# A two-layer relational graph convolution on one core: layer 1's projections issued in pieces between edge products, and transpositions issued one bunch after the copies they read

## The chip, the cores and the metric

The kernel runs on one core of one Trainium2 chip. The metric is the device time of one execution in microseconds (us). A few terms are used throughout. TensorE is PE in the profile, and PEld is its weight load; VectorE is DVE, ScalarE is ACT, GpSimd is POOL, and SyncE is SP. Each of these engines runs its own instructions strictly in the order in which the program issues them, so an instruction that waits holds back everything behind it on its engine.

## What is computed

There are 12,500 nodes with 128 features each and 200,000 edges sorted by destination. An edge has one of ten relations, the argmax of ten of its attributes. A layer averages the features of the sources over the edges of each (destination, relation) pair, multiplies the average by the relation's 128x128 matrix, sums over relations, and adds a root term and a bias:

```python
seg = dst * NUM_REL + edge_type
sums = segment_sum(x[src], seg); cnt = segment_sum(ones, seg)
mean = (sums / maximum(cnt, 1)).reshape(N, NUM_REL, -1)
return einsum('nrd,rdo->no', mean, w_rel) + x @ root + bias
```

The second layer takes the relu of the first one's result. The output is layernorm(x + layer 2). Everything is in float32.

## The kernel before, in words

**Tiles and bunches.** A tile is 128 edges; there are 1,563 of them (NT). Four tiles (QB) are a bunch, and layer 1's loop at L951 goes over bunches p. For each tile POOL gathers 128 source rows into a buffer `g` (L751); DVE compares keys with a table and writes a one-hot matrix `oh` (L765); ACT scales it by the edge weights (L757); PE multiplies `g` by `oh` into a PSUM tile `zp` (L986); DVE adds `zp` into the accumulator `cc` (L797), which is a ring of 1,024 node columns for each relation and each of two layers. In float32 one product is two PE passes, so the profile counts each twice.

**Both layers at once.** From tile T0 = 177 on, a gathered row holds the node's input features and, where it is already known, its layer-1 result: POOL gathers from one of two tables XH, and each tile is multiplied for both layers (16 passes a bunch). A block of nodes enters a table at an epoch. Epochs are whole multiples of RT = 11 tiles, and the first that lies at least READY = 8 bunches behind the block's finish is taken (L121), so it lies 8.0 to 10.5 bunches behind. The edges whose source is not known in time are done in layer 2 (L1290), which gathers from the finished table `hD`.

**Buffers.** There are 7 buffers `g`, so POOL may stand up to seven bunches ahead of PE. There are five `zp` tiles, two to a bunch. Everything else in PSUM shares two banks (`pf`).

**The order is written by hand.** `todo.at(t, f)` (L804) puts off a step to a later bunch; `todo.run(t)` at the end of a bunch (L1016) issues what is due. Within bunch p the program issues: `ones` of p+2 (DVE), the weights of p+1 (ACT), the gathers of p (POOL), the products of p (PE), pending preparation jobs, the sums of p-2 (DVE), then `finish(k)` for a block of 256 nodes that is now complete, then the steps that are due.

**Finishing a block in layer 1 (L844), about every eight bunches.** With p the bunch of finish, the steps are: in p, `projected` (L732), 11 matmuls of 256 columns, 22 PE passes in a row: ten relations (L739) and the root term (L742). In p+1, ACT copies the result with relu into `a` (L672, issued by L860), PE transposes `a` (L864), ACT copies the transposed rows to `hb` (L871), and SP stores them to `hD` and XH (L634); SP also fetches the next block's features. In p+2 and p+3 ACT clears the block's part of the ring (L722). At the end of p+3 PE runs the second layer's 22 passes; in p+4 ACT copies them to `v` (L891) and PE transposes the next block's features (L919); in p+5 ACT copies those (L926) and clears, and in p+6 it clears again.

**Finishing a block in layer 2 (L1394).** Time is counted in tiles i and a step unit u, which is 0.7 tile for the usual block of 256 nodes: the projection at i; at i+6u ACT's copy `a` (L1416) and, straight after it, PE's transposition (L1423); at i+10u the layernorm (L1427, first instruction L700) and the fetch for the next block.

Of the kernel before, what the change touches and what calls it, by code (L numbers as in the profile page):

```python
# [1 line left out]

# [62 lines left out]
def rgcn_resnorm_kernel(ctx: ExitStack, tc: tile.TileContext, x, src, dst, attr, w_rel1, root1, b1,  # L65
# [122 lines left out]
    def bounds(t):  # L188

        return max(0, t * STEP - OFF, floor_of(t)), min(N - 1, t * STEP + OFF)  # L190
# [541 lines left out]
    def projected(k, l, last, po=None, more=True, ring=None):  # L732
# [9 lines left out]
        nc.tensor.matmul(po[:, :n], w, f[:, :n], start=not more, stop=True)  # L742
        return po

    def stored(hb, b, k):

        rows_dma(hb, XH[b][:, C:], k, True)
# [89 lines left out]
    def layer_1():  # L837

        todo = Later()
        done = 0  # L840
        zps, ohs, xbs, fTs = {}, {}, {}, {}
        offs, row = None, None

        def finish(k, t):  # L844
# [9 lines left out]
            both = starts[k + 1] > bounds(T0)[0] if k + 1 < NBLK else True  # L854
            reused = starts[k] + RN < N
            assert not reused or t + 7 * u <= (starts[k] + RN - OFF - WN) // STEP

            def rows_out(_):
                a = po.pop()
                a = fin_a.setdefault(k, shifted(a, k, 0))  # L860
                pr = ps_f.tile([P, 4, C], F32, name="pf")
                n0, n, subs = block(k)
                for i, h in subs:
                    nc.tensor.transpose(pr[:h, i, :], a[:, i * P:i * P + h], ident)  # L864
                po.append(pr)

            def rows_kept(now):
                pr = po.pop()
                hb = fin.tile([P, 2, C], F32, name=f"hb{k % 2}")
                for p, s in spans(k):  # L870
                    nc.scalar.activation(hb[:p, s], pr[:p, s], AF.Copy)  # L871
                rows_dma(hb, hD, k, True)
                if k <= K1:
                    first = 0 if k <= K0 else (k - K0) % 2
                    free = first_seen[k - 1] - QB if k > K0 else 0
                    if now >= free:
                        stored(hb, first, k)
                    else:
                        todo_late.append((free, lambda t: stored(hb, first, k)))
                    if k < K1:  # L880
                        when = t + 8 * QB if k < K0 else first_seen[k] - QB
                        todo_late.append((when, lambda t: stored(hb, 1 - first, k)))

            def second(_):
                po.append(projected(k, 1, (rsb[1], fin_a.pop(k)), more=both))

            def second_kept(_):
                n0, n, _ = block(k)
                p2 = po.pop()
                t2 = fin.tile([P, 3 * P], F32, name="v")  # L890
                nc.scalar.activation(t2[:, :n], p2[:, :n], AF.Identity, bias=bsb[1])  # L891
                nc.sync.dma_start(T2[:, n0:n0 + n], t2[:, :n])

            todo.at(t + u, rows_out)
            todo.at(t + u, rows_kept)
            if reused:
                todo.at(t + 2 * u, lambda t: cleared(0, k, 0))
                todo.at(t + 3 * u, lambda t: cleared(0, k, 1))
            if k < NBLK - 1:
                todo.at(t + (9 if k >= NBLK - 3 else 3) * u, second)  # L900
                todo.at(t + (9 if k >= NBLK - 3 else 4) * u, second_kept)
            else:
                todo.run(t)
                todo.run(END)
                todo.at(t, second)
                todo.at(t, second_kept)
            if both:
                w = 10 if k >= NBLK - 3 else 5
                todo.at(t + w * u, lambda t: cleared(1, k, 0))
                todo.at(t + (w + 1) * u, lambda t: cleared(1, k, 1))  # L910
            if k + 1 < NBLK - 1:
                def fetch(t):
                    xbs[k + 1] = rows_in(k + 1)

                def turn(t):
                    n0, n, subs = block(k + 1)
                    pt = ps_f.tile([P, YB], F32, name="pf")
                    for i, h in subs:
                        nc.tensor.transpose(pt[:, i * P:i * P + h], xbs[k + 1][:h, i, :], ident[:h, :h])  # L919
# [31 lines left out]
        for p in range(-AHEAD, NPT + BEHIND):  # L951
# [27 lines left out]
            def products(g, oh, slot):  # L979
                t0, n = parts[p]  # L980
                zps[p] = [ps_z.tile([P, YB], F32, name="zp") for _ in range(0, n, 2)]
                for j in range(n):
                    i = t0 + j
                    zp, a = zps[p][j // 2], j % 2 * 2 * KW
                    for l in (0, 1) if i >= T0 else (0,):
                        nc.tensor.matmul(zp[:, a + l * KW:a + (l + 1) * KW], g[:, (slot[j] + l) * C:(slot[j] + l + 1) * C],  # L986
                                         oh[:, j * KW:(j + 1) * KW], start=True, stop=True)

            def sums():
                nonlocal done, offs, row  # L990
# [22 lines left out]
            if p == NPT - 1:  # L1013
                products(*made)
            made = None
            todo.run(t)  # L1016
# [4 lines left out]
        assert not todo_late and not jobs.due  # L1021

    if NCH > 1:
        sources(1)
# [265 lines left out]
    def layer_2():  # L1290
# [103 lines left out]
        def finish(k, i):  # L1394

            todo.run(END)
            fetched(k)
            ring = 1 - walk_of[k]
            n0, n, subs = block(k)
            u = (1 if n > YB * 5 // 8 else 0.7) if i < NG else 0  # L1400
            folded(slice(ring, ring + 1), k, max([b[6] for b, (lo, hi) in zip(bunches, reaches)
                                                  if b[0] == walk_of[k] and lo < n0 < hi] + [WN]))
            po = [projected(k, 1, (ident, fTs[k]), ring=ring)]
            following = turn_of[walk_of[k]]
            if k == partial:
                following = turn_of[1][1:2]
            else:
                following = following[following.index(k) + 1:][:1]
            if k == NB2 - 1:
                following = finals  # L1410
            elif following and following[0] in finals:
                following = []

            def turn(_):
                a = fin.tile([P, 3 * P], F32, name="a")
                nc.scalar.activation(a[:, :n], po.pop()[:, :n], AF.Copy)  # L1416
                if k == partial:
                    nc.sync.dma_start(T2[:, n0:n0 + n], a[:, :n])
                    fetched(following[0])
                    return  # L1420
                pr = ps_f.tile([P, 4, C], F32, name="pf")
                for b, h in subs:
                    nc.tensor.transpose(pr[:h, b, :], a[:, b * P:b * P + h], ident)  # L1423
                po.append(pr)

            def norm(_):
                normed(k, xbs[k], po.pop())  # L1427
                for f in following:
                    fetched(f)

            if k in finals:
                last_steps.extend((turn, norm))
# [12 lines left out]

        fetched(0)
        fetched(partial)
# [264 lines left out]
```

## Time and profile before

| what | value |
|---|---|
| median of 3 runs | 3830.8 us (3828.63 to 3833.66) |
| the profiled execution | 3870.04 us, its span 3868.2 us |
| granted TensorE clock, mean | 0.782 of full speed |
| busy share of the span | PE 63%, POOL 60%, DVE 53%, ACT 34% |
| layer 1 with both tables, 311 to 2406 us | 2095 us, 1,386 gathers |
| layer 2 with its own lists, 2697 to 3784 us | 1087 us, 691 gathers |

The profiled execution is 39 us longer than the median. A group's row gives busy time, mean duration of one in ns, and then the engine's idle time just before these instructions with what ended it. "remote" there, and "another core or an unknown queue" in the chain, stand for a wait whose end the profile cannot attribute.

### The profile page before, as it was taken

To read this page: it belongs to the slowest core of one execution; us is meant where nothing else is said; L and a number is where in the kernel's file an instruction comes from. 1 tells how busy PE (TensorE), PEld (TensorE's weight loads), DVE (VectorE), ACT (ScalarE), POOL (GpSimd) and SP (SyncE) were. 2 spreads that over 40 slices of the span, in tenths; PEclk is the share of its full clock that TensorE was granted. 3 is DMA by queue.
4 is the path that set the end of the run, shared out by engine and by line. 5 is a ranking of instruction groups with operands and counts; after the bars stand their busy time and mean duration, and the time that the engine had idled before them with its cause. 6 is when DMAs were issued, how large, how long until landed. Compare 5 with 4: busy or idle time off the path is not lost.

```text
span 3868.2 us, 42422 instructions
## 1 busy us (share of the span) xinstructions
PE 2449.6 (63%) x11862; PEld 2035.8 (53%) x11862; DVE 2030.8 (53%) x5475; ACT 1306.5 (34%) x3189; POOL 2301.8 (60%) x2443
## 2 busy tenths in 40 slices
PE   1535676767676767676667776245457676665667
PEld 0435665656565656566566666234434444454555
DVE  4435455655455656554444443187556555555565
ACT  1322333333333333333333333122324344444443
POOL 6645666666666666666566665655566666565650
PEclk7657787888888878788788788656678888888778
DMA  4663434343434343434343333211112222221221
GB/s 138 179 183 104 133 107 130 105 129 102 130 107 135 102 130 104 130 106 134 97 131 107 105 97 86 72 45 49 43 49 64 60 60 59 58 60 54 60 61 28
DMA packets 265342, 370.70 MB, mean 96 GB/s; under 512 B 51441, under 2 KB 197398, under 8 KB 265100
## 3 DMA queue, kind: packets, MB, share of 16 engines
q0 software_dynamic: 99968, 250.31, 23.4%
q1 hardware_dynamic: 111517, 91.95, 7.6%
q10 hardware_dynamic: 53615, 25.62, 2.3%
q8 instruction: 102, 1.67, 0.2%
q14 instruction: 140, 1.15, 0.1%
HBM read 322.58 MB, written 57.89 MB: 98 GB/s over the span
## 4 chain that ended last, share of the span: by engine, by line
PE 32%; another core or an unknown queue 22%; DVE 21%; issue 17%; ACT 4%; DVEq 2%; DMA 1%; POOL 1%; ACTq 0%; SPq 0%; POOLq 0%
PE zp L986 13%; PE pf L739 11%; DVE cc L797 8%; PE zp L1505 2%; ACT oh L757 2%; DVE oh L775 2%; DVE oh L765 2%; PE zq L1505 1%; DVEq L782 1%; PE pf L742 1%; PE pf L1197 1%; POOL g L751 1%; ACT cc L722 1%; DVE eqb L548 1%
## 5 line engine op out<-in xcount | busy, mean ns | idle before, releaser
L751 POOL DMA_INDIRECT g<-XH,idxE x1386 | 1311.3, 946 | 815.7 <-issue 387.6
L797 DVE TENSOR_TENSOR cc<-cc,zp 128x240 f32 (+12 forms) x2190 | 836.3, 382 | 1023.7 <-remote 604.5
L986 PE MATMUL zp<-oh,g 128*128 128x120 f32 x5898 | 983.6, 325 | 552.6 <-issue 382.7
L986 PEld LDWEIGHTS zp<-oh,g 128*128 128x128 f32 x5898 | 913.7, 236 | 621.5 <-issue 441.2
L751 POOL DMA_INDIRECT g<-hD,idxB x691 | 653.0, 945 | 433.1 <-issue 194.1
L739 PE MATMUL pf<-cc,w 128*128 128x256 f32 (+5 forms) x3000 | 762.8, 412 | 138.3 <-issue 61.4
L739 PEld LDWEIGHTS pf<-cc,w 128*128 128x128 f32 x3000 | 612.6, 217 | 269.7 <-issue 94.8
L757 ACT ACTIVATE oh<-oh,wE 128x120 f32<-128x120 f32 x1740 | 533.2, 382 | 225.2 <-DVE oh L765 124.0
L757 ACT ACTIVATE oh<-oh,wB 128x150 f32<-128x150 f32 (+23 forms) x771 | 337.9, 481 | 410.4 <-DVE oh L775 198.3
L1505 PE MATMUL zp<-oh,g 128*128 128x120 f32 (+22 forms) x1254 | 341.7, 417 | 211.1 <-DVE cc L797 89.1
L1505 PEld LDWEIGHTS zp<-oh,g 128*128 128x128 f32 x1254 | 239.9, 240 | 289.5 <-issue 239.6
L722 ACT ACTIVATE cc<-zero 128x1280 f32<-128x1280 f32 (+1 forms) x274 | 336.2, 1229 | 74.8 <-DVE cc L797 57.6
L775 DVE TENSOR_TENSOR oh<-wide,keyB 128x480 f32<-128x480 f32 (+19 forms) x402 | 228.8, 569 | 228.8 <-remote 156.0
L672 ACT ACTIVATE a<-pf,b 128x256 f32<-128x256 f32 (+1 forms) x50 | 23.3, 466 | 812.6 <-remote 570.8
L765 DVE TENSOR_TENSOR oh<-bank,keyE 128x480 f32<-128x480 f32 x391 | 253.1, 647 | 0.0
L1505 PE MATMUL zq<-oh,g 128*128 128x140 f32 (+20 forms) x642 | 193.2, 435 | 87.3 <-DVE cc L797 32.7
L751 POOL DMA_INDIRECT g<-hD,idxE x177 | 168.6, 953 | 121.9 <-issue 49.7
L751 POOL DMA_INDIRECT g<-in_x_dram,idxE x177 | 167.3, 945 | 110.0 <-issue 50.8
L1505 PEld LDWEIGHTS zq<-oh,g 128*128 128x128 f32 x642 | 127.2, 234 | 134.5 <-issue 88.2
L797 DVE TENSOR_TENSOR cc<-cc,zq 128x150 f32 (+20 forms) x321 | 124.0, 386 | 55.1 <-PE pf L739 21.3
L891 ACT ACTIVATE v<-pf,b 128x256 f32<-128x256 f32 (+2 forms) x52 | 24.0, 461 | 320.0 <-remote 100.7
L548 DVE TENSOR_TENSOR eqb<-bank,kh 128x1344 bf16<-128x1344 f32 (+2 forms) x65 | 100.5, 1549 | 28.1 <-remote 22.3
(241 smaller groups left out, 1296.2 us busy)
## 6 DMA issues: line engine op xcount, KB each, us to landing
m<-in_edge_attr_dram SPq DMA_DIRECT2D x48, 672.0 KB
g<-XH,idxE POOLq DMA_INDIRECT x1386
XH<-in_x_dram ACTq DMA_DIRECT2D x24, 512.0 KB
XH<-zero ACTq DMA_DIRECT2D x24, 512.0 KB
XH<-hb SPq DMA_DIRECT2D x87, 128.0 KB
g<-hD,idxB POOLq DMA_INDIRECT x691
xb<-in_x_dram SPq DMA_DIRECT2D x72, 128.0 KB
hD<-hb SPq DMA_DIRECT2D x46, 128.0 KB
```

Source lines behind the costliest of these rows:

```text
L548: nc.vector.tensor_tensor(eq[:p], kpP[:p, None, :R].to_broadcast([p, DB, R]), fore, op=ALU.is_equal)
L722: nc.scalar.activation(cc[:, l, h * H:(h + 1) * H, o:o + n], zero[:, None, :n].to_broadcast([P, H, n]), AF.Copy)
L739: nc.tensor.matmul(po[:, :n], wsb[l][:, r, :], cc[:, l if ring is None else ring, r, o:o + n], start=(r == 0), stop=False)
L742: nc.tensor.matmul(po[:, :n], w, f[:, :n], start=not more, stop=True)
L751: nc.gpsimd.indirect_dma_start(out=g[:, j * C:(j + n) * C], out_offset=None, in_=table, in_offset=bass.IndirectOffsetOnAxis(ap=idx, axis=0))
L757: nc.scalar.activation(s, s, AF.Copy, scale=w)
L765: nc.vector.tensor_tensor(o.rearrange("p (t m) -> p t m", m=m), cols[:, None, :m].to_broadcast([P, n, m]), keys[:, :, None].to_broadcast([ ...
L775: nc.vector.tensor_tensor(to, a, b, op=ALU.is_equal)
L782: vals = nc.values_load_multi_w_load_instructions(row, engines=[DVE], min_val=min(a for a, _ in lims), max_val=max(b for _, b in lims), sk ...
L797: nc.vector.tensor_tensor(s, s, z, op=ALU.add)
L986: nc.tensor.matmul(zp[:, a + l * KW:a + (l + 1) * KW], g[:, (slot[j] + l) * C:(slot[j] + l + 1) * C], oh[:, j * KW:(j + 1) * KW], start=Tr ...
L1505: nc.tensor.matmul(zp[:, j * m:(j + 1) * m], gt[:, b * C:(b + 1) * C], oh[:, j * m:(j + 1) * m], start=True, stop=True)
```

## The change

No instruction is added or taken away; instructions change places on PE, ACT, SP and DVE.

- Layer 1's projections (both layers' parts, for every block that is kept for two layers except the last three) are cut into 11 pieces of two passes. Three are issued where all 11 stood. Of the rest, two each go behind the first and the second tile's products of the next bunch, and the last four at that bunch's end, ahead of its due steps.
- In layer 1 the copy `a` stays in p+1, but the transposition, the copy to `hb` and the stores move from p+1 to p+2 (not for the last block but one). The transposition of the next block's features moves from p+4 to p+5, and its copy from p+5 to p+6.
- In layer 2 the copy stays at i+6u, the transposition moves to i+8u, and the layernorm from i+10u to i+11u.

```diff
+    def projection(k, l, last, po, more=True):
+        n0, n, _ = block(k)
+        o = n0 % RN
+        def piece(r):
+            if r is None:
+                w, f = last()
+                nc.tensor.matmul(po[-1][:, :n], w, f[:, :n], start=not more, stop=True)
+            else:
+                if not r:
+                    po.append(ps_f.tile([P, YB], F32, name="pf"))
+                nc.tensor.matmul(po[-1][:, :n], wsb[l][:, r, :], cc[:, l, r, o:o + n], start=(r == 0), stop=False)
+        return [piece_of(piece, r) for r in [*range(NREL), None]]
...
+        def beside(pieces, t):
+            now = 3 if t + 2 * QB < NT else len(pieces)
+            for f in pieces[:now]:
+                f()
+            if pieces[now:]:
+                side[t // QB + 1] = pieces[now:]
...
-            po = [projected(k, 0, (rsb[0], fTs[k]))]
+            apart = both and k < NBLK - 3
+            if apart:
+                po = []
+                beside(projection(k, 0, lambda: (rsb[0], fTs[k]), po), t)
+            else:
+                po = [projected(k, 0, (rsb[0], fTs[k]))]
...
+            def rows_copied(_):
+                a = po.pop()
+                fin_a[k] = shifted(a, k, 0)
+
             def rows_out(_):
-                a = po.pop()
-                a = fin_a.setdefault(k, shifted(a, k, 0))
+                a = fin_a[k]
...
-            def second(_):
+            def second(t):
+                if apart:
+                    beside(projection(k, 1, lambda: (rsb[1], fin_a.pop(k)), po), t)
+                    return
...
-            todo.at(t + u, rows_out)
-            todo.at(t + u, rows_kept)
+            todo.at(t + u, rows_copied)
+            todo.at(t + (1 if k == NBLK - 2 else 2) * u, rows_out)
+            todo.at(t + (1 if k == NBLK - 2 else 2) * u, rows_kept)
...
-                w = 2 if k == NBLK - 3 else 4
+                w = 2 if k == NBLK - 3 else 5
                 todo.at(t + w * u, turn)
                 todo.at(t + (w + 1) * u, turned_kept)
...
+                pieces = side.pop(p, [])
                 for j in range(n):
...
+                    if j < 2:
+                        for f in [pieces.pop(0) for _ in range(min(2, len(pieces)))]:
+                            f()
+                left.extend(pieces)
...
             made = None
+            while left:
+                left.pop(0)()
             todo.run(t)
...
-            def turn(_):
+            def copied(_):
                 a = fin.tile([P, 3 * P], F32, name="a")
                 nc.scalar.activation(a[:, :n], po.pop()[:, :n], AF.Copy)
...
+                po.append(a)
+
+            def turn(_):
+                a = po.pop()
                 pr = ps_f.tile([P, 4, C], F32, name="pf")
...
-            todo.at(min(i + 6 * u, by), turn)
+            todo.at(min(i + 6 * u, by), copied)
...
-                todo.at(i + 10 * u, norm)
+                todo.at(i + 8 * u, turn)
+                todo.at(i + 11 * u, norm)
```

More of the change, by code (lines that the diff above doesn't have):

```diff
@@ L1 @@
 from contextlib import ExitStack
+from functools import partial as piece_of
 import concourse.bass as bass
@@ L840, in layer_1 @@
         done = 0
-        zps, ohs, xbs, fTs = {}, {}, {}, {}
+        zps, ohs, xbs, fTs, side = {}, {}, {}, {}, {}
         offs, row = None, None
+        left = []
+        def beside(pieces, t):
[3 more added lines that the diff above has]
+            if pieces[now:]:
+                assert t // QB + 1 not in side
+                side[t // QB + 1] = pieces[now:]
         def finish(k, t):
             if k < NBLK - 2:
+                while left:
+                    left.pop(0)()
                 todo.run(END)
@@ L852, in finish @@
             folded(ALL, k, WN)
-            po = [projected(k, 0, (rsb[0], fTs[k]))]
             both = starts[k + 1] > bounds(T0)[0] if k + 1 < NBLK else True
+            apart = both and k < NBLK - 3
+            assert not apart or t + 4 * QB < NT
+            if apart:
[3 more added lines that the diff above has]
+                po = [projected(k, 0, (rsb[0], fTs[k]))]
             reused = starts[k] + RN < N
             assert not reused or t + 7 * u <= (starts[k] + RN - OFF - WN) // STEP
+            def rows_copied(_):
+                a = po.pop()
+                fin_a[k] = shifted(a, k, 0)
             def rows_out(_):
-                a = po.pop()
-                a = fin_a.setdefault(k, shifted(a, k, 0))
+                a = fin_a[k]
                 pr = ps_f.tile([P, 4, C], F32, name="pf")
@@ L1015, in layer_1 @@
             made = None
+            while left:
+                left.pop(0)()
             todo.run(t)
@@ L1020, in layer_1 @@
         todo.run(END)
-        assert not todo_late and not jobs.due
+        assert not todo_late and not jobs.due and not side
     if NCH > 1:
@@ L1431, in finish @@
             if k in finals:
-                last_steps.extend((turn, norm))
+                last_steps.extend((copied, turn, norm))
                 if k == finals[1]:
```

## The prediction

> **What bounds the kernel now.** I read the page's busy times first, then the chain that ended last.
>
> ```profile
> span 3868.2 us, 42422 instructions
> PE 2449.6 (63%) x11862; PEld 2035.8 (53%) x11862; DVE 2030.8 (53%) x5475; ACT 1306.5 (34%) x3189; POOL 2301.8 (60%) x2443
> PE 32%; another core or an unknown queue 22%; DVE 21%; issue 17%; ACT 4%; DVEq 2%; DMA 1%; POOL 1%; ACTq 0%; SPq 0%; POOLq 0%
> PE zp L986 13%; PE pf L739 11%; DVE cc L797 8%; PE zp L1505 2%; ACT oh L757 2%; DVE oh L775 2%; DVE oh L765 2%; PE zq L1505 1%; DVEq L782 1%; PE pf L742 1%; PE pf L1197 1%; POOL g L751 1%; ACT cc L722 1%; DVE eqb L548 1%
> ```
>
> No engine is full, and the chain wanders between PE, DVE and releasers that the trace cannot name. The change touches two stages, so I cut them out by windows (window and length, then busy time with instructions of PE, PEld, DVE, ACT and POOL, granted clock, DMA share, GB/s).
>
> ```profile
> 311.00:2406.00 2095.00, 1455.42 (x7866) 1271.02 (x7867) 1060.96 (x2814) 670.56 (x1740) 1310.76 (x1386) 0.82 0.39 115
> 2697.00:3784.00 1087.00, 694.76 (x2631) 514.85 (x2629) 614.97 (x1788) 450.43 (x956) 653.02 (x692) 0.79 0.21 57
> ```
>
> In the first, which is layer 1 for both tables, PE is busy for 1455 of 2095 us (69%). POOL shows 1311 us, but its sequencer needs time between two gathers. What POOL waited for in this window (total us, times, longest):
>
> ```profile
> POOL g L751 <- issue: 387.6, 1205, 3.5
> POOL g L751 <- remote: 215.9, 100, 3.9
> POOL g L751 <- PE zp L986: 87.1, 37, 6.7
> POOL g L751 <- DMA XH<-hb: 35.6, 8, 9.0
> POOL g L751 <- DMA XH<-zero: 31.9, 1, 31.9
> POOL g L751 <- PE pf L742: 21.2, 11, 2.6
> POOL g L751 <- PE pf L864: 16.0, 4, 9.6
> POOL g L751 <- PE pf L559: 7.2, 5, 1.9
> POOL g L751 <- PE pf L269: 7.1, 3, 3.0
> POOL g L751 <- PE pf L919: 2.6, 1, 2.6
> ```
>
> The issue row is 1,205 gaps of 0.32 us. Busy time and issue together are 1698 us, 81% of the stage: POOL is the nearest thing to a bound, and the other 397 us are its pauses. 141.2 us of them (the five rows that name PE) wait for PE to release a `g`; 215.9 us end at something unnamed; 35.6 us wait for a block's rows to reach the table XH. In layer 1, therefore, a change of PE's order is worth only what it takes from, or adds to, these pauses. PE's own idle time costs nothing as long as POOL does not pause for it.
>
> **A, the projections in pieces.** One block in the timeline (start, length, engine, line, idle time before and its releaser):
>
> ```profile
> 1204.36 6.77 PE L739 MATMUL pf<-cc,w 128*128 128x256 f32 x20
> 1211.40 1.94 PE L986 MATMUL zp<-oh,g 128*128 128x120 f32 x16
> 1221.91 0.94 POOL L751 DMA_INDIRECT g<-XH,idxE  x1 [2.95 <-remote]
> 1222.01 0.69 PE L864 MATMUL pf<-ident,a 128*128 128x128 f32 x2 [8.68 <-DVE cc L797]
> 1227.86 4.48 PE L739 MATMUL pf<-cc,w 128*128 128x256 f32 x20
> 1249.47 3.74 PE L986 MATMUL zp<-oh,g 128*128 128x120 f32 x16 [0.95 <-issue]
> ```
>
> The 20 relation passes take 4.48 to 6.77 us in a row, where a bunch's 16 products take 1.94 to 3.74 us; POOL behind the burst paused for 2.95 us. The change spreads 88 such projections (two of each of 44 blocks). No pass is saved. Of 22 passes 14 now stand ahead of or between the next bunch's products and 8 behind them, so that these products end 8/22 = 36% of a burst earlier. What pauses do the bursts cause? The rows that name a projection or the transposition behind it are 21.2 + 16.0 = 37.2 us, 26% of the 141.2 us. If the unnamed pauses have the same share, 0.26 x 215.9 = 57 us, all bursts together cost 94 us. I take 36% of that: **-34 us**, with the bounds 0 and -94. Seven buffers `g` speak for the low end, since 5.0 us of gathers a bunch can run ahead of a burst; they are full wherever POOL waits for PE.
>
> **B, ACT's order.** These rows price what moves.
>
> ```profile
> L739 PE MATMUL pf<-cc,w 128*128 128x256 f32 (+1 forms) x1760 | 453.3, 412 | 47.0 <-issue 32.5 <-ACT v L891 9.1 <-DVE oh L765 1.2
> L722 ACT ACTIVATE cc<-zero 128x1280 f32<-128x1280 f32 (+1 forms) x169 | 210.3, 1246 | 55.3 <-DVE cc L797 49.3 <-issue 6.0
> L864 PE MATMUL pf<-ident,a 128*128 128x128 f32 x87 | 24.6, 373 | 107.0 <-DVE cc L797 73.3 <-ACT a L672 13.5 <-issue 11.7
> L919 PE MATMUL pf<-ident,xb 128*128 128x128 f32 x87 | 19.6, 309 | 14.3 <-ACT v L891 10.6 <-DVE cc L797 3.6
> PE zp L986 <- ACT oh L757: 66.1, 29, 5.5
> ```
>
> With the copy `hb` moved to p+2, it and the clear (1.25 us) stand together ahead of the weights of a bunch that PE will multiply next. PE waited for such weights 29 times in some 346 bunches, 8%. 44 blocks x 8% x 1.25 us is **+5 us**; the bounds are 0 (ACT is busy for 32% of the stage and catches up) and 44 x 1.25 = +55.
>
> PE's 107.0 us ahead of the transposition (L864) look like the prize, but I price them at nothing. Before, the burst ends bunch p, the products of p+1 follow, and then the transposition waits for the copy `a`. After, the last four pieces end bunch p+1, the products of p+2 follow, and then comes the transposition. One bunch of products stands between, now as then. What these waits cost POOL is the row of 16.0 us, which is in A's bound. The copy's own order does not change: `a` stays behind the same products.
>
> **C, the table XH.** `hb` and its stores come a bunch of products later: 1.94 us at full clock to 3.74 us, in the mean 2.9 us. Does a gather stand behind that? Blocks of rows enter the table 8.0 to 10.5 bunches behind their finish. By the kernel's own lists 14 of the 41 epochs lie under 9 bunches behind, and the pauses are found with these. Three of them, with the windows of 32 gathers around them and three windows of 32 without one:
>
> ```profile
> 1321.02 0.95 POOL L751 DMA_INDIRECT g<-XH,idxE  x1 [6.74 <-PE zp L986]
> 1853.30 0.95 POOL L751 DMA_INDIRECT g<-XH,idxE  x1 [8.73 <-DMA XH<-hb]
> 2188.46 0.95 POOL L751 DMA_INDIRECT g<-XH,idxE  x1 [9.01 <-DMA XH<-hb]
> ```
>
> ```profile
> 1793.50:1839.80 46.30, 32.94 (x192) 30.05 (x190) 30.51 (x80) 15.80 (x40) 30.36 (x32) 0.82 0.46 136
> 1827.30:1881.50 54.20, 37.02 (x196) 32.12 (x195) 27.56 (x66) 16.83 (x44) 30.55 (x32) 0.78 0.34 96
> 1262.30:1309.50 47.20, 36.54 (x208) 30.73 (x207) 31.33 (x92) 15.58 (x40) 30.27 (x32) 0.89 0.37 104
> 1298.00:1349.10 51.10, 35.45 (x187) 30.42 (x188) 27.71 (x81) 15.57 (x40) 30.27 (x32) 0.77 0.35 97
> 2128.60:2174.70 46.10, 35.67 (x188) 30.79 (x188) 19.16 (x46) 15.95 (x41) 30.25 (x32) 0.79 0.36 103
> 2162.30:2216.60 54.30, 36.19 (x168) 29.84 (x167) 24.23 (x59) 15.69 (x40) 30.25 (x32) 0.73 0.37 104
> ```
>
> The three waits, less the usual 0.30, are 23.6 us; their windows are 7.9 + 3.9 + 8.2 = 20.0 us longer than those without. So 85% of such a wait becomes time. 14 blocks x 2.9 us x 0.85 is **+35 us**. The bounds are 0 (the stores land in time) and a whole bunch of the stage, 2095 us / 346.5 = 6.05 us, for the 16 epochs that lie up to 9 bunches behind: 97 us.
>
> **D, the next block's features.** PE's 14.3 us ahead of L919 are mostly a wait for the copy `v` (10.6), which a bunch of distance covers. PE is not the bound, so I take a third: **-5 us**, bounds 0 and -14. The copy `fT` is needed only at the next finish, two bunches later.
>
> **E, layer 2.** Here copy and transposition stood back to back, and PE waited.
>
> ```profile
> PE pf L1423 <- ACT a L1416: 82.1, 15, 12.9
> L700 DVE TENSOR_TENSOR v<-pf,xb 128x256 f32<-128x256 f32 x20 | 8.4, 420 | 35.7 <-PE pf L1423 13.3 <-PE zp L1505 9.7 <-remote 7.6
> ```
>
> Two steps u are 1.4 tiles, at 1087 us / 691 gathers = 1.57 us a tile 2.2 us. 15 waits x 2.2 us = 33 us go from PE's path. Some of these waits are 12.9 us long and only shrink, and what is late next is PE's wait for DVE's sums, so I take half: **-16 us**, bounds 0 and -82. The layernorm keeps 3 steps u instead of 4 behind the transposition; DVE already idles 35.7 us there, which bounds the loss at +36.
>
> **The sum** is -34 + 5 + 35 - 5 - 16 = -15 us: layer 1 stays as it is (+1), layer 2 gains 16. The profiled execution is 3870.0 us, 39.2 us above the median of the runs shown; I carry the difference over: 3830.8 - 15 = **3816 us**.
>
> **The rivals.**
>
> R1, slower: the stores decide. If the stores slip a whole bunch of the loop, with PE's transposition held behind products that themselves wait and ACT's `hb` behind them, all 16 epochs pay 6.05 us x 0.85 = +82; the bursts are worth half of my figure (-17). With B, D and E as above: 82 - 17 + 5 - 5 - 16 = +49, **3880 us**. It turns to a loss from a delay of 50 / (14 x 0.85) = 4.2 us, as all other terms sum to -50. For it speaks that XH waits up to 9.0 us already exist; against it, that most epochs lie over 9 bunches behind.
>
> R2, no change: only the pauses that name a burst are its doing. A is 36% of 37.2, -13: the sum is +6, **3837 us**. The many unnamed releasers speak for this: a pause that begins after PE is done is not cured by a smoother PE.
>
> R3, much faster: the bursts start all their pauses and a step of distance cures layer 2's waits (A -94, E -33): -94 + 5 + 35 - 5 - 33 = -92, **3739 us**. Against it: the seven buffers.
>
> R4, slower by the clock. The same 20 passes took 6.77 us in one place and 4.48 us in another, with a granted clock of 0.82 for the stage: the pace of PE varies. If cutting the bursts puts all 88 projections at the slower pace, that is 2.29 x 88 = 201 us of PE; at PE's 32% of the chain, +64 us, and the sum is +49: **3880 us**. Against it: PE's busy share does not change, and single passes between products leave no new gap. The Trainium skill, "TensorE: Matmul & The Clock Gate", section "HAM oscillation — how this bites in real kernels", holds that idle gaps of more than about 3.4 us halve PE's rate again and advises to keep its work together, which would favour the burst. The trace leaves that open: the slow products of 3.74 us show only 0.95 us of idle time ahead of them.
>
> That the change does not do what it says is no rival: in the instruction order of the changed program the pieces, transpositions and copies stand where the diff puts them.
>
> **How the numbers follow.** The forecast has 0.36, with 3786 to 3823 as its own range (A from -27 to -64 with the rest as taken), R1 0.30, R2 0.14, R3 0.12, R4 0.08. About 0.2%, 7.7 us, is what a measurement can tell from no change. Faster is forecast and R3, 0.48; within it R2, 0.14; slower R1 and R4, 0.38. The range, 3755 to 3895, takes in the forecast, R2 and most of R1 and R4 (each some 15 us to either side), and leaves out R3 and their tails.
>
> **What would show it.** In layer 1's POOL waits, A: the rows naming L742 and L864 fall from 37 us by about a third, and the unnamed one with them. C: the row of XH<-hb rises from 35.6 us (8 waits) to some 70. B: PE's wait for ACT's weights stays near 66. D: PE's wait for `v` ahead of L919 goes. PE's idle time ahead of L864 stays near 107. E: the wait for L1416 falls from 82 to about 49, and layer 2 is some 16 us shorter. I am wrong if layer 1's length moves by more than 50 us, or if PE's passes change their mean of 412 ns.

## The result

| | median us | lowest to highest | runs |
|---|---|---|---|
| before | 3831.43 | 3828.63 to 3833.66 | 7 |
| after | 3844.97 | 3840.07 to 3849.43 | 7 |

The change costs 13.5 us: the ratio is 1.0034, with a 95% interval of 1.0024 to 1.0044. The forecast was 3816 us, 15 us faster: 3845 us lies inside its range of 3755 to 3895 us, but the sign is wrong. In a second comparison (run after_again below) the same two kernels took 3865.84 and 3893.89 us: ratio 1.0074 (1.0059 to 1.0088), 28 us slower.

Two things have to be known before the profiles are compared. The levels of separate comparisons differ, here by 34 us for the kernel before, so a kernel is judged only against the runs of the kernel before in its own comparison. And the profile of before shown above took 3870.0 us, 39 us over the median that goes with it, but only 4 us over the 3865.84 of the second comparison. I therefore set it beside the profile of after_again (3886.76 us, where the runs' median is 3893.89) and not beside the first profile of after (3840.07 us).

The windows of the same two stages in after_again, from the first to the last gather out of XH and from layer 2's first to its last gather (columns as before):

```profile
303.00:2430.80 2127.80, 1491.38 (x7854) 1279.83 (x7854) 1056.53 (x2803) 659.98 (x1724) 1310.85 (x1386) 0.81 0.39 113
2725.00:3801.30 1076.30, 697.14 (x2628) 514.78 (x2626) 614.07 (x1781) 449.58 (x955) 652.53 (x691) 0.79 0.22 57
```

POOL's 1,386 gathers take the same 1311 us, but the stage is 2127.8 us long and was 2095. Layer 2's gathers take 1076.3 us and took 1085.7 (2697.35 to 3783.08). So the loss is in layer 1, in what POOL waits for (from 311 us on, so that the wait for the first table, 32.5 us until 303 us, is not among the rows):

```profile
POOL g L768 <- issue: 398.5, 1213, 6.6
POOL g L768 <- remote: 227.0, 96, 4.5
POOL g L768 <- PE zp L1028: 113.3, 46, 11.3
POOL g L768 <- DMA XH<-hb: 64.0, 13, 10.6
POOL g L768 <- PE pf L754: 4.8, 3, 2.4
POOL g L768 <- PE pf L901: 2.2, 2, 1.9
...
POOL g L768 <- PE pf L758: 1.4, 1, 1.4
```

The rows that name the projection (L754 and L758 now) and its transposition (L901) have shrunk from 37.2 us to 8.4 us, as the change would have it, while the products' own row has grown from 87.1 to 113.3 us and the unnamed one from 215.9 to 227.0. The row of the tables has grown from 35.6 us in 8 waits to 64.0 us in 13. The names are only the last releasers, so I also took the pauses by place: for every gather of this stage the idle time ahead of it less 0.31 us, from the trace's list of gathers. At the first gathers of the 41 epochs they sum to 90 us before and 140 us in after_again (49 more); everywhere else to 302 and 287 (15 less). Of the 49 us, 28 lie at the 14 epochs that are under 9 bunches behind (83 us for 55), 21 at the 26 others (24 for 3) and 1 at the first one, where POOL waits for the new table (32 in both). The longest pause behind the first table's belonged to the epoch of the prediction's row at 1853.30 us, where it was 8.73 us:

```profile
1870.44 0.95 POOL L768 DMA_INDIRECT g<-XH,idxE  x1 [10.63 <-DMA XH<-hb]
```

Why the rows come later can be seen in one block of after_again, at the place where the prediction showed the burst of before. Some rows of PE, the copies and the store are shown; `...` stands for rows left out.

```profile
1205.32 1.47 PE L758 MATMUL pf<-cc,w 128*128 128x256 f32 x6
...
1210.73 0.70 PE L758 MATMUL pf<-cc,w 128*128 128x256 f32 x2 [0.33 <-issue]
...
1211.45 0.60 PE L1028 MATMUL zp<-oh,g 128*128 128x120 f32 x4
...
1211.89 1.04 PE L758 MATMUL pf<-cc,w 128*128 128x256 f32 x4
...
1212.76 1.05 PE L1028 MATMUL zp<-oh,g 128*128 128x120 f32 x8
...
1213.65 1.47 PE L758 MATMUL pf<-cc,w 128*128 128x256 f32 x6
...
1214.95 0.59 PE L754 MATMUL pf<-fT,root 128*128 128x256 f32 x2
...
1223.35 0.47 ACT L673 ACTIVATE a<-pf,b 128x256 f32<-128x256 f32 x1 [19.76 <-remote]
...
1223.88 0.69 PE L901 MATMUL pf<-ident,a 128*128 128x128 f32 x2 [2.98 <-ACT a L673]
...
1224.91 0.38 ACT L908 ACTIVATE hb<-pf 128x256 f32<-128x256 f32 x1
...
1225.74 0.46 SPq L635 DMA_DIRECT2D XH<-hb  x1
```

In before, the root term that ends the burst of the prediction's row at 1204.36 us, and the copy behind it:

```profile
1210.96 0.59 PE L742 MATMUL pf<-fT,root 128*128 128x256 f32 x2
...
1221.49 0.47 ACT L672 ACTIVATE a<-pf,b 128x256 f32<-128x256 f32 x1 [23.05 <-remote]
```

In after_again the projection's first pass starts at 1205.3 and its last one (the root term) ends at 1215.5: the whole next bunch lies inside it. In before the burst began at 1204.4 and ended at 1211.5. The copy `a` reads the last pass, so it now follows the end of bunch p+1. Over the 41 blocks that have an epoch, from the trace's lists of these instructions: the mean time from the last product of bunch p to the copy `a` is 12.4 us before and 16.0 us in after_again (1.3 and 6.3 us behind the last product of p+1); the mean time from the last gather of bunch p to the first store into XH is 46.0 and 49.1 us.

### The profile page after: what moved, and what is told of

It reads as the page before. It is cut to its first block, busy times and chain, and to the rows that moved or that the text cites. A ratio compares the mean times of both kernels' runs of the same rounds, so it can differ in the third digit from the quotient of the medians.

```text
span 3838.2 us, 42453 instructions
## 1 busy us (share of the span) xinstructions
PE 2485.1 (65%) x11862; PEld 2036.8 (53%) x11862; DVE 2031.1 (53%) x5475; ACT 1299.9 (34%) x3189; POOL 2300.0 (60%) x2443
## 4 chain that ended last, share of the span: by engine, by line
PE 35%; DVE 19%; issue 18%; another core or an unknown queue 18%; ACT 6%; DVEq 2%; POOL 1%; DMA 1%; ACTq 0%; SPq 0%; POOLq 0%
PE zp L1028 15%; PE pf L758 8%; DVE cc L814 7%; PE pf L740 5%; ACT oh L774 3%; PE zp L1558 2%; DVE oh L792 2%; ACT cc L723 2%; POOL g L768 1%; DVE oh L782 1%; PE zq L1558 1%; DVEq L799 1%; PE pf L754 1%; DVE cc L1213 1%
## 5 line engine op out<-in xcount | busy, mean ns | idle before, releaser
L1028 PE MATMUL zp<-oh,g 128*128 128x120 f32 x5898 | 1016.6, 322 | 555.6 <-issue 416.8
L1028 PEld LDWEIGHTS zp<-oh,g 128*128 128x128 f32 x5898 | 938.5, 233 | 674.6 <-issue 497.1
L758 PE MATMUL pf<-cc,w 128*128 128x256 f32 (+1 forms) x1760 | 526.1, 430 | 107.8 <-issue 59.0
L758 PEld LDWEIGHTS pf<-cc,w 128*128 128x128 f32 x1760 | 358.6, 224 | 171.6 <-issue 81.2
L1558 PEld LDWEIGHTS zp<-oh,g 128*128 128x128 f32 x1254 | 240.9, 241 | 311.7 <-issue 220.5
L740 PE MATMUL pf<-cc,w 128*128 128x256 f32 (+7 forms) x1240 | 316.5, 419 | 86.8 <-DVE cc L814 36.7
```

What stands on the lines that cost most here:

```text
L740: nc.tensor.matmul(po[:, :n], wsb[l][:, r, :], cc[:, l if ring is None else ring, r, o:o + n], start=(r == 0), stop=False)
L758: nc.tensor.matmul(po[-1][:, :n], wsb[l][:, r, :], cc[:, l, r, o:o + n], start=(r == 0), stop=False)
L1558: nc.tensor.matmul(zp[:, j * m:(j + 1) * m], gt[:, b * C:(b + 1) * C], oh[:, j * m:(j + 1) * m], start=True, stop=True)
```

## The experiments

Two theories were set against each other. **S**: what costs is that a block's rows reach XH later, so that the first gather of an epoch waits. **P**: cutting the projections costs by itself, in the order of PE or ACT. A third, **L**, looked for the loss in layer 2. Each kernel was timed in five rounds beside the kernel before; its ratio is to the runs of before in the same comparison.

### The parts, first time

Layer 2's part alone was the changed kernel with

```diff
-            apart = both and k < NBLK - 3
+            apart = False
-            todo.at(t + (1 if k == NBLK - 2 else 2) * u, rows_out)
-            todo.at(t + (1 if k == NBLK - 2 else 2) * u, rows_kept)
+            todo.at(t + u, rows_out)
+            todo.at(t + u, rows_kept)
-                w = 2 if k == NBLK - 3 else 5
+                w = 2 if k == NBLK - 3 else 4
```

> Layer 2's part of the change alone (copy at i+6u, transposition at i+8u, layernorm at i+11u); layer 1 as before. Theory S (the stores to XH that come a bunch later cost what the other parts gain, and more): layer 2 gains its estimated 16 us, 3815. Theory P (cutting the projections is what costs): 3815 too. Theory L (the later layernorm and the lost distance to the next block are what costs): 3840 or more.

Layer 1's part alone took back layer 2's timing:

```diff
-                todo.at(i + 8 * u, turn)
-                todo.at(i + 11 * u, norm)
+                todo.at(min(i + 6 * u, by), turn)
+                todo.at(i + 10 * u, norm)
```

> Layer 1's part of the change alone (pieces, later transpositions and stores); layer 2 as before. Theory S and theory P: the whole loss and layer 2's gain on top, 3831 + 13 + 16 = 3860. Theory L: 3831 or less.

The pieces alone kept `apart` and took back all the rest, which is the last two changes of the first diff and the whole second one:

> Only the projections in pieces: copy, transposition, copy to hb and stores all in p+1 behind the last piece, so that the transposition again waits for its copy. Theory S: no later stores than before by more than the last eight passes, 3820 to 3835. Theory P: 3850 to 3860.

And the later transpositions alone set `apart = False` and took back layer 2's timing:

> Only layer 1's transpositions a bunch later (block's rows, with copy hb and stores, and the next block's features); projections in one burst, layer 2 as before. Theory S: +35 to +45, about 3870. Theory P: 3825 to 3835, since the transposition no longer waits for its copy.

All four missed, in the same way. They took 3087.93, 3089.84, 3090.07 and 3088.79 us, and the kernel before took 3089.07 us beside them (ratios 0.9996, 1.0005, 1.0007 and 0.9999, and each interval takes in 1). Everything, the kernel before included, was 742 us faster here than in the first runs. The waits of POOL in l2_only, in the stage with the tables, show why:

```profile
POOL g L768 <- issue: 381.7, 1253, 0.3
POOL g L768 <- PE zp L1028: 24.4, 80, 0.3
POOL g L768 <- DMA g<-XH,idxE: 9.4, 31, 0.3
```

No wait is longer than 0.3 us: POOL never pauses, and the stage's window is its gathers, 1,386 at 1.25 us:

```profile
225.30:1958.60 1733.30, 1432.66 (x7943) 1241.34 (x7944) 1058.77 (x2820) 667.61 (x1733) 1311.37 (x1386) 0.85 0.47 138
```

With POOL as a bound that never waits, no order on the other engines can show. To see whether the chip or the kernels had done it, the changed kernel itself was run again.

> The changed kernel itself again. In the four runs before, POOL issued a gather every 1.25 us without a pause and all kernels took 3088 to 3090 us, 742 us less than the kernel before in its first profile. If that was the kernels' doing, this one takes 3845 us. If it was the chip's (PE's semaphore increments are seen 0.01 us after they are made there, and several us late in the first profiles), it takes 3086 to 3092 us where the kernel before takes 3089, or 3845 where the kernel before takes 3831.

It took 3893.89 us beside 3865.84 (the second comparison above), so it was not the kernels. The difference is in when PE's signals are seen. ACT was idle ahead of the copy `a` of all 41 blocks that have an epoch: it began the copy 0.04 us (median) behind the projection's last pass in l2_only, and 5.1 us behind it in the profile of before. ACT's own signals were prompt in both: SP's store to `hD` starts 0.02 to 0.03 us (medians) behind the end of `hb`. The trace's records of semaphore increments show the same. In the stage with the tables, the first record at or behind the last product of a bunch comes 0.01 us after it in l2_only (median; 90% quantile 0.02); in before the median is 2.1 us and the 90% quantile 6.7 us, in after_again 1.7 and 7.2 us. These quantiles are upper estimates, since the record of before holds 1,975 of PE's 2,311 increments on this semaphore and that of l2_only 2,304 of 2,311. Why the delay differs from one time on the chip to another, the runs do not tell; chip 1 of the record gave 3089 us here and 3829 us in the last comparison below, and the kernel before changes with it in the same way. Everything below concerns the condition with late signals, in which the change was measured.

### The parts again

> Only layer 1's transpositions, copies hb and stores a bunch later, on another chip, since the first four runs had no pauses of POOL at all. Two profiles of chips with pauses show them at the first gather of an epoch rise by 49 us and all others fall by 15. Theory S (the later stores): this kernel has the whole rise and not the fall, 35 to 50 us over the kernel before. Theory P (the pieces): at most 5 over. On a chip without pauses: no difference.

> Only the pieces, everything else in layer 1 issued where it was. Theory S: stores later by the last eight passes and one wait for the copy, +10 to +15, less the 15 us of other pauses: -5 to +5. Theory P: 20 to 30 over the kernel before. On a chip without pauses: no difference.

The third kernel of this group is new: the first projection keeps its burst and its transposition, only the second one, whose result goes to `T`, is cut. The later transposition of the next block's features and layer 2's part stay as in the change.

```diff
-            if apart:
+            if apart and False:
                 po = []
                 beside(projection(k, 0, lambda: (rsb[0], fTs[k]), po), t)
...
-            todo.at(t + (1 if k == NBLK - 2 else 2) * u, rows_out)
-            todo.at(t + (1 if k == NBLK - 2 else 2) * u, rows_kept)
+            todo.at(t + u, rows_out)
+            todo.at(t + u, rows_kept)
```

> A new order: only the second layer's projection (at p+3, nothing of it goes to XH) in pieces; the first one in one burst and its transposition, hb and stores at p+1 as before; next features and layer 2 as in the change. Theory S: stores are where they were, half of the relief is kept: 5 to 15 us under the kernel before. Theory P: half of the loss, 10 to 15 over. On a chip without pauses: no difference.

> Layer 2's part alone again. The profiles of before and after differ by 2 us over the last 600 gathers of layer 2, so both theories: 0 to 6 us under the kernel before; the forecast's -16 if PE's wait for its copy were on the path. On a chip without pauses: no difference.

The kernel before took 3868.06 us. later_only_b took 3869.17 (ratio 1.0003, interval 0.9991 to 1.0014), spread_only_b 3894.25 (1.0063, 1.0048 to 1.0078), second_spread 3867.75 (0.9992, 0.9981 to 1.0004), l2_only_b 3869.80 (1.0002, 0.9993 to 1.0011). So the whole loss is in the pieces, and the second projection's pieces neither cost nor gain: it is the first projection's. For later_only_b and spread_only_b the forecasts of P came true and both of S failed; for second_spread both theories missed. As S was put, with the transposition's bunch as the cause, it is wrong, since later_only_b should have cost 35 to 50 us. What it did to PE is instructive. PE's waits ahead of the two transpositions in later_only_b, complete:

```profile
PE pf L901 <- issue: 3.6, 7, 0.8
PE pf L960 <- issue: 2.2, 3, 1.1
```

The 107.0 us ahead of the block's transposition, 2.4 us for each of 44 blocks, are gone, and the time is the same. PE comes to the transposition without stalling, and so the bunch of distance puts the stores only 0.8 us later (46.8 us behind the gather for 46.0), not 2.9. The pieces do more (47.6 us), and both together most (49.1 us).

The zero of later_only_b is itself a sum. Its first gather out of XH starts at 301.8 us, where it starts at 311.5 us in before and at 312.9 in l2_only_b, so some 10 us are gained ahead of the tables; its pauses at epochs are 101 us for 90 and 93. S therefore holds in small here, and the gain ahead of the tables hides it.

### The first projection alone, and epochs that come later

The first projection's pieces alone, which is spread_only with

```diff
-                if apart:
+                if False:
                     beside(projection(k, 1, lambda: (rsb[1], fin_a.pop(k)), po), t)
```

> Only the first layer's projection in pieces, all else as before. Both pieces spread cost 26 us, the second one's nothing with the rest. Theory S: the first one's result goes to XH and comes 3.6 us later, so the whole +20 to +26 is here. Theory M (the loss comes from two sets of pieces in the same eight bunches): about +10.

The other two kernels change one number, in the kernel before and in the changed one:

```diff
-READY = 8
+READY = 9
```

The 14 epochs that lay less than 9 bunches behind their block's finish come one step of 11 tiles later; what they can no longer give goes to layer 2 (694 gathers there in place of 691).

> The kernel before with READY = 9 in place of 8: the 14 epochs that lay under 9 bunches behind their block's finish come 11 tiles later, the other 27 stay; some 400 edges go to layer 2 for it (estimate: 3 tiles of 1.57 us, +5 us). Theory S (the gathers of early epochs wait for the stores): most of the 55 us of pauses at these 14 epochs goes, 20 to 40 us under the kernel before. Theory F (POOL would pause anyway, for PE's late releases): 0 to +5.

> The changed kernel with READY = 9. Theory S: the loss over its own base shrinks; it lies 0 to 12 us over the kernel before with READY = 9, since the 27 other epochs keep their rise (35 to 60 us in pauses) and the other pauses fall by 15. Theory P (the pieces cost by themselves, in PE's or ACT's order): still 26 over the kernel before with READY = 9.

The kernel before took 3831.32 us. first_spread took 3862.79 us (1.0090, 1.0072 to 1.0108), so the first projection's pieces carry the loss alone; theory M falls, though 31 us is more than the 20 to 26 that S gave. With READY = 9 the kernel before took 3818.06 us (0.9966, 0.9953 to 0.9979) and the changed kernel **3805.32 us** (0.9929, 0.9912 to 0.9946). With READY = 8 the change lost 13 to 28 us; with READY = 9 it gains 13. A cost that lay wholly in PE's or ACT's order would have stayed. The row of the tables among POOL's waits, in the kernel before with READY = 9 and then in the changed kernel with it:

```profile
POOL g L751 <- DMA XH<-hb: 0.3, 1, 0.3
```

```profile
POOL g L768 <- DMA XH<-hb: 17.2, 7, 5.9
```

By place, the pauses at epochs are 57 and 65 us, and some 33 us of each is the wait for the first table, which READY does not move. At the 14 early epochs the changed kernel pauses for 2 us, where it was 83 in after_again. The sizes were missed even so: the kernel before gained 13 us where S expected 20 to 40 and F none, and theory S expected the change to lie 0 to 12 us over its base here, and it lies 13 us under it.

The two traces tell where these 13 us come from. The first gather out of XH, in the kernel before with READY = 9 and in the changed one:

```profile
312.50 0.94 POOL L751 DMA_INDIRECT g<-XH,idxE  x1 [34.60 <-DMA XH<-in_x_dram]
```

```profile
299.97 0.95 POOL L768 DMA_INDIRECT g<-XH,idxE  x1 [33.08 <-DMA XH<-zero]
```

So 12.5 us are gained ahead of the tables. The stage with the tables is still longer, 2063.6 us for 2053.4, where it was 33 us longer in after_again; layer 2's gathers and what follows them take 11 us less, which is no more than layer 2's stage moves from profile to profile. In all five slower-level profiles with READY = 8 or 9 that have the later transpositions the first gather out of XH starts at 300 to 303 us; in the five with neither these nor a single projection cut, it starts at 311 to 313. In between are first_spread (303.4 us) and second_spread (307.4), so the transpositions' place need not be the only cause. READY = 9 thus takes away most of the loss in the tables' stage, and what then shows is a gain in another place, which the forecast did not have.

### What the pieces cost without early epochs

Three more kernels combine READY = 9 with the pieces alone and with the later transpositions alone, and READY = 11 with the whole change.

> Only the pieces (as in spread_only_b), with READY = 9. The kernel before with READY = 9 had 0.9966 of the kernel before's time, the change with it 0.9929. Theory S: without early epochs the pieces cost nothing, 0.995 to 0.999 of the kernel before. Theory P: they cost their 0.6% here too, 1.003.

> Only layer 1's later transpositions (as in later_only_b), with READY = 9. In the profiles the kernels that have them save some 10 us between gathers 130 and 180, where PE no longer holds POOL. Theory S: that saving shows, 0.993 to 0.995 of the kernel before. If they save nothing, as in later_only_b: 0.9966.

> The whole change with READY = 11: every epoch lies at least 11 bunches behind, the tables start 11 tiles later, and some 900 edges more go to layer 2 than with READY = 9 (estimate: 7 tiles, 11 us, and as much again for the later start). Theory S: the last 32 us of pauses at epochs, times 0.85, go, so it is within 10 us of the change with READY = 9, 0.991 to 0.995. Theory P: about 10 to 20 us slower than with READY = 9, 0.996 to 0.999.

This time there were no pauses again, with the kernel before at 3089.26 us: 3088.89 us (0.9997), 3090.72 (1.0005) and 3100.66 (1.0038, 1.0024 to 1.0052). They tell one thing: the added work of READY = 11, whose tables start 11 tiles later, costs 11 us. Once more:

> The pieces alone with READY = 9 once more, as the last chip had no pauses. Theory S: 0.995 to 0.999 of the kernel before (the kernel before with READY = 9 had 0.9966). Theory P: 1.003. On a chip without pauses: no difference.

> The later transpositions alone with READY = 9 once more. If they save 10 us ahead of the tables: 0.993 to 0.995 of the kernel before; if nothing: 0.9966. On a chip without pauses: no difference.

> The whole change with READY = 11 once more. On the chip without pauses it took 11 us more than the kernel before, which is its added work. Theory S: the 27 us of epochs' pauses that READY = 9 leaves go against that work: 0.989 to 0.995 of the kernel before (with READY = 9 it had 0.9929). Theory P: 0.996 to 0.999. On a chip without pauses: 1.004 again.

Beside 3828.86 us of the kernel before, spread_ready9_b took 3830.09 (0.9995, 0.9979 to 1.0011), later_ready9_b 3820.28 (0.9978, 0.9963 to 0.9993) and after_ready11_b 3823.32 (0.9981, 0.9967 to 0.9994). Both ranges of S, for the pieces and for READY = 11, were missed, the first narrowly; READY = 11 fell in P's. The later transpositions saved no more than READY = 9 alone. Within one comparison the ratio of the pieces alone was 0.60% over that of the later transpositions alone with READY = 8, and 0.17% with READY = 9, where the two intervals overlap. In each pair 9 to 11 us lie ahead of the tables (the first gather out of XH at 312.9 and 301.8 us, 310.9 and 301.9), which with READY = 9 is as much as the whole difference. So most of what the pieces cost is what the early epochs waited for; whether a rest is a cost of their own stays open. READY = 11 did not take the epochs' pauses away. There `free` (L912), which lets a block into a table only once an earlier epoch no longer needs it, puts 37 of the 41 first stores into p+3 to p+5, by the kernel's own lists, and the epochs pause for 57 us, 24 of them at the first table. Of the kernels timed at this level, the changed one with READY = 9 has the lowest ratio.

By place, from each trace (means and sums in us; delay of `a` behind the last product of bunch p, delay of the store behind the last gather of bunch p, and the two kinds of pauses):

| kernel | `a` | store | pauses at epochs | other pauses | ratio |
|---|---|---|---|---|---|
| before | 12.4 | 46.0 | 90 | 302 | 1 |
| second_spread | 11.8 | 45.9 | 89 | 304 | 0.9992 |
| l2_only_b | 12.6 | 46.1 | 93 | 309 | 1.0002 |
| later_only_b | 13.5 | 46.8 | 101 | 309 | 1.0003 |
| spread_only_b | 15.0 | 47.6 | 115 | 298 | 1.0063 |
| first_spread | 16.4 | 48.0 | 120 | 289 | 1.0090 |
| after (first profile) | 15.5 | 48.4 | 137 | 264 | 1.0034 |
| after_again | 16.0 | 49.1 | 140 | 287 | 1.0074 |
| before_ready9 | 11.7 | 46.8 | 57 | 294 | 0.9966 |
| later_ready9_b | 13.2 | 47.6 | 62 | 297 | 0.9978 |
| spread_ready9_b | 15.3 | 49.0 | 52 | 315 | 0.9995 |
| after_ready9 | 15.3 | 50.0 | 65 | 294 | 0.9929 |
| after_ready11_b | 15.0 | 59.7 | 57 | 299 | 0.9981 |

In the rows with READY = 8 the later the store, the more the epochs pause. In those with READY = 9 the stores come as late, and the epochs mind less: without the first table's wait, 20 to 32 us. A single profile's sums move by some 10 us between kernels that do the same in layer 1 (before and l2_only_b), and the ratios of different comparisons can differ by 0.4%, as the two of the changed kernel show; ratios of different comparisons in the last five rows are not to be compared more finely.

## Why the prediction was wrong

**What bounds the kernel: right.** POOL's pauses decide layer 1. PE's stalls ahead of its transpositions disappeared without any effect on the sum (later_only_b), and where POOL had no pauses, no change of order mattered. A slip without weight: six rows, not five, name PE in the 141.2 us.

**A, the projections in pieces: this step failed.** It asked what the cut projection leaves behind the next bunch's products (8 passes of 22) and what they then release earlier, and took the burst's own result to be unhurried. Some relief is there: pauses away from the epochs fall by 15 us in after_again, for the -34 forecast. Of its signs, the rows that name a burst fell further than by a third (37.2 to 8.4 us), but the unnamed row did not fall with them (215.9 to 227.0). But the result is complete only with its last pass, and that moved from the end of bunch p to the end of bunch p+1. The copy `a` follows 3.6 us later. The prediction said "The copy's own order does not change: `a` stays behind the same products." That is so in the instruction order, and yet it missed eight passes that now stand behind these products and ahead of the copy. About half of the copy's delay goes on to XH: 1.6 of 2.6 us in spread_only_b, 2.0 of 4.0 in first_spread. Of the second projection nothing waits for the last pass, and there the pieces cost nothing (second_spread). PE's idle time ahead of L864, forecast to stay near 107 us, fell to 35.2 us in after_again.

**C, the table XH: the mechanism right, its source and size wrong.** The forecast took 2.9 us of delay from the transposition's place and 35 us of time. The runs show 0.8 us from the transposition's place, 1.6 to 2.0 us from the pieces alone, and 3.1 us from both. The pauses at epochs rise by 49 us, at the prediction's 85% 42 us. The 14 early epochs that it counted have 28 of these 49; 21 lie at later ones, which its figure of +35 put at nothing. It forecast that the row of XH<-hb would rise from 35.6 to some 70 us; it rose to 64.0. With the measured sizes, 42 for C and -13 for A, and nothing for B, D and E, the sum is +29 in place of -15; the comparison that goes with this profile measured +28. That they meet to 1 us is luck, since a profile's sums move by some 10 us.

**B, ACT's order: no cost seen.** PE's waits for weights sum to 64.8 us in after_again, 66.1 before, though in 43 waits for 29.

**D, the next block's features: failed.** The wait for `v` ahead of L960 is gone from the list, but PE's idle time there is not: 17.9 us of issue and 5.3 us for DVE stand for the 14.3 us of before. later_only_b holds this edit too and gained nothing in sum.

**E, layer 2: failed in size.** PE's wait for the copy fell as forecast, and further, from 82.1 us. Among PE's waits in layer 2 of after_again:

```profile
PE pf L1475 <- ACT a L1464: 39.2, 10, 12.3
```

Yet layer 2's part alone measured 1.0002 (0.9993 to 1.0011), so the -16 us are zero to within 4 us. Its gathers take 1065 to 1090 us in the slower-level profiles that have this part and 1068 to 1086 us in those without it. The prediction had applied to layer 1 that idle time of PE is free, and priced the same kind of idle time at half its length in layer 2.

**The rivals.** R1 named the mechanism, the stores, and its place, but with the wrong cause (the transposition behind waiting products) and, at +49, too high a price. Its threshold, a delay of 4.2 us, was too high as well: with A and E at their measured sizes 3.1 us were enough. R2's price for A, -13 us, is the size that was found, but its sum of +6 kept C at 35 and E at -16. R3 did not occur. R4 is not needed: the pieces' passes average 425 ns for 412 (3% more), and the second projection's pieces did not move the time. What R4 left open, the trace of before tells: the granted clock was 1.00 during the products of 1.94 us and the burst of 4.48 us, 0.50 during the products of 3.74 us and 0.66 during the burst of 6.77 us. The clock had thus changed with the bursts whole. The Trainium skill, "TensorE: Matmul & The Clock Gate", section "HAM oscillation — how this bites in real kernels", holds that idle gaps of more than about 3.4 us throttle PE again; the granted clock of layer 1's stage is 0.81 in after_again and was 0.82, so no run here shows that cutting the work adds to this.

## What to carry to other kernels

Cutting a block of work into pieces between other work helps what stands behind the block and delays what reads its result. Before cutting, ask for each result who reads it and how much time that reader has: here the same cut was free on the projection whose reader had time, and cost up to 0.9% on the one whose rows a gather was waiting for. And when a delay eats a gain, look for the deadline that it meets: one constant, which put 14 of 41 deadlines 11 tiles later, turned the loss of 0.3 to 0.7% into a gain of 0.7%. About half of that gain the constant gave to the kernel before as well (0.34%), and the rest, by the traces, comes from another place than the one that was in view. So take a difference apart by place before it is put down to one cause.

## What the runs showed of the hardware

The same program ran at two levels, 3089 us and 3829 to 3868 us. At the faster level ACT began a copy that waited for PE 0.04 us (median) behind PE's last pass and POOL issued a gather every 1.25 us without a pause, with layer 1's stage at 1733 us (l2_only); at the slower one ACT began the same copy 5.1 us behind PE's last pass (median of 41), while signals of ACT itself stayed prompt, and the same stage took 2095 us (before). The granted clock, at 0.85 in that stage for 0.82, is a small part of this: PE's busy time there is 1433 us for 1455. A change of order could be seen only at the slower level. What sets the level, no run here shows.
